# Leftover taps, distances and leftover coefficients regrouped on TensorE, and the batch norms' rows moved by one round, in a two-layer graph network kernel

## The chip, the cores and the metric

The kernel runs on one core of one Trainium2 chip. A core has five engines with instruction streams of their own: TensorE (PE, matrix products; its weight loads are shown as PEld), VectorE (DVE), ScalarE (ACT), GpSimd (POOL) and SyncE (SP, which here only issues DMAs). [...] The metric is the device time of one execution in microseconds; less is better. Everything is computed in float32, and each float32 product shows in the trace as two passes, so a "x2" in a row of TensorE is one product of the program.

## The reference

Two layers over 128 graphs of 128 nodes with 256 features each:

```python
# layer 0, per graph
norm  = (adj.sum(-1) + 1e-6) ** -0.5
f_hom = norm * (adj @ (norm * (x @ theta)))
gate  = sigmoid(x @ W_t + b_t)
x = layernorm(x + elu(gate * f_hom + (1 - gate) * (x @ W_h)))
# layer 1, with adj as a mask of weights
h = relu(bn1(conv1(x.T)))                  # kernel size 1
h = bn2(conv1d(h, conv2_w, pad=8))         # 17 taps along the nodes
x_conv = relu(h + x.T).T
s = x @ w_se.T + b_se                      # 3 coordinates per node
dist = |s_n|^2 + |s_m|^2 - 2 s_n . s_m
x_nmp = (exp(-dist) * adj) @ relu(x @ w_msg.T + b_msg)
x = layernorm(x + gru(concat(x_conv, x_nmp), x))
```

## The kernel before

The graphs are taken in 64 pairs and later in 32 groups of four (`G = 4`). The 17-tap convolution is done by a real Fourier transform of length 136: analysis of `h` with a 128x136 table `A`, one product over the features per frequency, and synthesis back. Of the 136 coefficients the first 128 fill the array's rows and the last `ML = 8` are "leftovers" that are kept apart everywhere: `S` is the 128x128 way back and `SL` the one of the leftovers.

**Stage A** (0 to about 740 us) walks over the pairs in rounds `t`, software-pipelined: in round `t` `l0_project` of pair `t`, the gate and the norm of pair `t-1`, `l1_turn` and `l1_front` of `t-2`, `l1_analyse` of `t-3`, `l0_turn` of `t+1`, `l0_mix` of `t`. In every second round it also transforms a part of the convolution's weights: `w_unit(u)` loads two features in each of four 32-row groups (17 taps in 32 rows), multiplies each group by the table `T` (four products `w_ps`, L416, which stand in four separate row groups of the array), and makes the 8 leftover coefficients of all four groups by one more product over all 128 rows, `wl_ps` (L419), with a block-diagonal table `TL`. VectorE copies the leftovers out (L425). `w_store` writes all of it to `w_d` in DRAM a round later, eight DMAs for the main part (L433) and eight of 8 KB for the leftovers (L438), all on SP's queue. From round 3 on the order of PE, SP, DVE and ACT is the program's own; in rounds up to 2 only PE's is, and a scheduler orders the others.

In round 0 `batch_norms` transposes the norms' vectors (`vec_ps`), makes scale and shift (POOL takes the power), builds diagonal matrices (L227), spreads them over all partitions by one product (`row_ps`, L229) and scales `conv1_w` with it. `table` makes `A` and `T` on VectorE. `way_back` in round 1 makes `S`, `SL` and `TL`. POOL also computes each pair's reciprocal square roots: `inv_sqrt` (L161, L162), for the degrees and for the layer norms (`rstd_a`), in one queue.

**Stage B** (about 740 to 921 us) loops over 68 pairs of coefficients: it loads 512 KB of `w_d` per step (`wb`, L647), makes `y_ps` (L652) and `z_ps` (L665), and writes `y_d`. `others` prepares the next stage's constants in between, among them `mask`.

**Stage C** (from 921 us) walks over the 32 groups `g`: `l1_gather(g)` (the messages, `nmp_ps`), for `g+1` `l1_own` (POOL writes a masked copy `own` of 128x512, L814, from the transposed distance factors `turned`) and `l1_project` (`msg_ps`), `l1_gru(g, 0)`, then `l1_kernel(g+1)` (one product `dist_ps` of 128 rows by 512 columns, L824, its exponential on ACT, L828, and the product with the adjacency on VectorE, L829), in every second step `l1_synth` of the next two groups, and `l1_gru(g, 1)`. `l1_synth` makes 16 products with `S` (L752) and then 16 with the leftovers (L760, 8 rows each, in four row groups side by side), into four banks of the pool `acc`; VectorE takes them out (L769). `l1_gru` has seven `product`s of six passes of 384 columns (L899), in the order 0, 1, 5, 6, 4, 3, 2, each into one of four banks of the pool `psC`. PE's order is the program's; the other engines' is the scheduler's.

Of the kernel before, what the change touches and what calls it, by code (L numbers as in the profile page):

```python
# [14 lines left out]
P = 128  # L15
# [7 lines left out]
GD = P // KD  # L23
PAD = TAPS // 2
# [9 lines left out]
def gnn_layers_kernel(ctx: ExitStack, tc: tile.TileContext, a: dict, out: bass.AP):  # L34
# [54 lines left out]
    TL = taps.tile([P, 4 * ML], F32, tag="TL", name="TL")  # L89
# [9 lines left out]
    io = apool("io", 4, reuse_waits="tile")  # L99
    wk = apool("wk", 1, reuse_waits="tile")  # L100
    wf = apool("wf", 1, reuse_waits="tile")
    ps = actx.enter_context(tc.tile_pool(name="psA", bufs=8, space=PSUM, reuse_waits="tile"))
# [51 lines left out]
    for t in wt:  # L154
        nc.vector.memset(t, 0.0)
# [57 lines left out]
    def batch_norms():  # L213
        n = 2 * NC
        tv = bank("vec_ps")
        nc.tensor.transpose(tv[:, 0 : 4 * n], vec, ident[0 : 4 * n, 0 : 4 * n])
        col = setup.tile([P, 4 * n], F32, tag="col", name="col")
        nc.vector.tensor_copy(col, tv[:, 0 : 4 * n])
        inv_sqrt(scale, col[:, 0:n], BN_EPS, n)
        nc.vector.tensor_mul(scale, scale, col[:, 2 * n : 3 * n])  # L220
        nc.vector.tensor_mul(shift, col[:, n : 2 * n], scale)
        nc.vector.tensor_sub(shift, col[:, 3 * n : 4 * n], shift)

        diag = setup.tile([P, n, P], F32, tag="diag", name="diag")
        for i, v in enumerate((scale, shift)):
            for c in range(NC):
                nc.vector.tensor_scalar(diag[:, NC * i + c, :], ident, v[:, c : c + 1], None, ALU.mult)  # L227
        tr = bank("row_ps")
        nc.tensor.matmul(tr, lhsT=ones, rhs=diag.rearrange("p a b -> p (a b)"), start=True, stop=True)  # L229
        nc.vector.tensor_copy(shift1, tr[:, D : 2 * D])  # L230
        for c in range(NC):
            nc.vector.tensor_mul(conv1_w[:, c, 0:D], conv1_w[:, c, 0:D], tr[:, 0:D])

    def way_back():

        AL = setup.tile([P, P], F32, tag="AL", name="AL")
        nc.gpsimd.memset(AL, 0.0)
        nc.gpsimd.memset(TL, 0.0)
        back = setup.tile([P, 1], F32, tag="back", name="back")
        nc.vector.memset(back, 2.0 / L)  # L240
        nc.vector.memset(back[0:2], 1.0 / L)
        for r, (lo, hi) in enumerate(quarters):
            nc.vector.tensor_copy(TL[lo:hi, r * ML : (r + 1) * ML], T[lo:hi, P:M])
            nc.vector.tensor_copy(AL[:, lo : lo + ML], A[:, P:M])
        tS = bank("S_ps")
        nc.tensor.transpose(tS[:, 0:P], A[:, 0:P], ident)
        nc.tensor.transpose(tS[:, P : 2 * P], AL, ident)
        nc.vector.tensor_scalar(S, tS[:, 0:P], back, None, ALU.mult)
        nc.vector.tensor_scalar(SL, tS[:, P : 2 * P], 2.0 / L, None, ALU.mult)
# [126 lines left out]
    def l1_front(p):  # L376
        s = st[p]
        h = s["h"] = wf.tile([P, J, D], F32, tag="h", name=f"h_{p}")
        for j in range(J):
            ph = bank(f"conv1_ps_{p}_{j}")  # L380
            for c in range(NC):
                nc.tensor.matmul(  # L382
                    ph[:, 0 : D + CO], lhsT=s["x1T"][:, c, nodes(j)], rhs=conv1_w[:, c, :],
                    start=(c == 0), stop=(c == NC - 1),
                )
            nc.vector.tensor_tensor(h[:, j, :], ph[:, 0:D], shift1, ALU.add)
            nc.scalar.activation(coords[:, p * J + j, :], ph[:, D : D + CO], AF.Copy)
        nc.scalar.activation(h, h, AF.Relu)
# [22 lines left out]
    def w_unit(u):  # L411
        t = wt[u % NW].rearrange("p i o -> p (i o)")
        pq = [bank(f"w_ps_{u}_{r}") for r in range(4)]
        for r in range(4):
            k = slice(32 * r, 32 * r + TAPS)
            nc.tensor.matmul(pq[r], lhsT=T[k, 0:P], rhs=t[k, :], start=True, stop=True)  # L416
        pl = bank(f"wl_ps_{u}")
        wo = s_w[u] = []
        nc.tensor.matmul(pl[0 : 4 * ML, :], lhsT=TL, rhs=t, start=True, stop=True)  # L419
        for r in range(4):  # L420
            o = taps.tile([P, 2, D], F32, tag="wo", bufs=4, name=f"w_o_{u}_{r}")
            nc.scalar.activation(o.rearrange("p i o -> p (i o)"), pq[r], AF.Copy)
            wo.append(o)
        ol = taps.tile([4 * ML, 2, D], F32, tag="wl", name=f"wl_o_{u}")
        nc.vector.tensor_copy(ol.rearrange("p i o -> p (i o)"), pl[0 : 4 * ML, :])  # L425
        wo.append(ol)

    def w_store(u, between=lambda: None):
        *wo, ol = s_w.pop(u)
        for r in range(4):  # L430
            f = r * QF + 2 * u
            for i in range(2):
                nc.sync.dma_start(w_d[0 : P // 2, f + i, :, :], wo[r][:, i, :])  # L433
        between()
        for r in range(4):
            f = r * QF + 2 * u
            for i in range(2):
                nc.sync.dma_start(w_d[P // 2 : M // 2, f + i, :, :], ol[r * ML : (r + 1) * ML, i, :])  # L438
# [32 lines left out]
    units = {2 + u * (NP - 3) // (NU - 1): u for u in range(NU)}  # L471
    hstack = ExitStack()
    H = None
    E = mybir.EngineType
    for t in range(-1, NP):
        with tc.manual_schedule(engines={E.PE, E.SP, E.DVE, E.Activation} if t > 2 else {E.PE}):
# [15 lines left out]
            if t == 0:  # L492
                batch_norms()
                table(A, node, "A")
                table(T, lag, "T")

                cos, sin = T[:, 2:M:2], T[:, 3:M:2]
                both = setup.tile([P, M // 2 - 1], F32, tag="both", name="both")
                nc.vector.tensor_sub(both, sin, cos)
                nc.vector.scalar_tensor_tensor(sin, sin, -1.0, cos, ALU.mult, ALU.subtract)  # L500
                nc.vector.tensor_copy(cos, both)
# [7 lines left out]
            if t - 1 in units:  # L509
                w_store(units[t - 1])  # L510
            on(t + 1, l0_turn)
            if t == 3:
                nc.scalar.dma_start(w_msg, a["w_msgT"].rearrange("(c p) e -> p c e", p=P))
                nc.scalar.dma_start(b_msg, a["L1_gnn_b_msg"].partition_broadcast(P))
            if t == 1:
                way_back()
# [3 lines left out]
            on(t, l0_mix)  # L520
            if t in units:
# [5 lines left out]
    with tc.manual_schedule(engines={E.PE, E.SP, E.DVE, E.Activation}):  # L527
# [10 lines left out]
        w_store(units[last], lambda: m_load(3))  # L538
# [35 lines left out]
    mask = cw.tile([P, GD], F32, tag="mask", name="mask")  # L574
# [4 lines left out]
    def others():  # L579
# [18 lines left out]

        mask_i = cw.tile([P, GD], I32, tag="mask_i", name="mask_i")
        nc.gpsimd.iota(mask_i, pattern=[[-KD, GD]], base=0, channel_multiplier=1)  # L600
        mask_f = cw.tile([P, GD], F32, tag="mask_f", name="mask_f")
        nc.vector.tensor_copy(mask_f, mask_i)
        nc.vector.tensor_scalar(mask, mask_f, 0.0, None, ALU.is_ge)
        nc.vector.scalar_tensor_tensor(mask, mask_f, float(KD - 1), mask, ALU.is_le, ALU.mult)
# [79 lines left out]
    acc = cpool("acc", 4, space=PSUM)  # L684
# [44 lines left out]
    def load_y(d):  # L729

        yl = cy.tile([P, G, P], F32, tag="yl", bufs=2, name=f"yl_{d}")
        for e in range(2):
# [3 lines left out]
            for c in range(NC):  # L736
                r = NC * e + c
                nc.sync.dma_start(
                    yl[32 * r : 32 * r + ML],
                    y_d[g * G : (g + 1) * G, P:M, c * P : (c + 1) * P].rearrange("q m f -> m q f"),  # L740
# [4 lines left out]
    def l1_synth(d):  # L745
        pcs = {}
        for e in range(2):
            s = st[2 * d + e]
            for c in range(NC):
                pc = pcs[e, c] = acc.tile([P, 512], F32, tag="acc", name=f"conv2_ps_{2 * d + e}_{c}")  # L750
# [5 lines left out]
        for q in range(G):  # L756
            for e in range(2):
                for c in range(NC):
                    k = slice(32 * (NC * e + c), 32 * (NC * e + c) + ML)
                    nc.tensor.matmul(  # L760
                        pcs[e, c][:, nodes(q)], lhsT=sy[2 * d + e][1][k, q, :], rhs=SL[k, :],
                        start=False, stop=(q == G - 1), skip_group_check=True,
                    )
# [36 lines left out]
    def l1_own(g):  # L800
        if g % (GD // G) == 0:
# [10 lines left out]
        own = ck.tile([P, G, P], F32, tag="own", name=f"own_{g}")  # L812
        lo = g * G % GD
        nc.gpsimd.tensor_tensor(  # L814
            own, turned[:, 1, :].unsqueeze(1).to_broadcast([P, G, P]),
            mask[:, lo : lo + G].unsqueeze(2).to_broadcast([P, G, P]), ALU.mult,
# [3 lines left out]
    def l1_kernel(g):  # L820
        s = st[g]
        turned, own = s["turned"], s["own"]
        pd = bankc(f"dist_ps_{g}")
        nc.tensor.matmul(  # L824
            pd, lhsT=turned[:, 0, :], rhs=own.rearrange("p q n -> p (q n)"), start=True, stop=True
        )
        AT = ck.tile([P, G * P], F32, tag="AT", name=f"AT_{g}")
        nc.scalar.activation(AT, pd, AF.Exp, scale=-1.0)  # L828
# [62 lines left out]
    def l1_gru(g, pr):  # L891
# [3 lines left out]

        def product(i):
            pg = bankc(f"g_ps_{g}_{pr}_{i}")
# [44 lines left out]
    with tc.manual_schedule(engines={mybir.EngineType.PE}):  # L942
# [6 lines left out]
        for g in range(2):  # L949
            l1_project(g)  # L950
        for g in range(2):
            l1_kernel(g)
        l1_factors()
        l1_synth(0)
        for g in range(NG):
# [11 lines left out]
            if 2 <= g + 1 < NG:  # L967
                l1_kernel(g + 1)
            if g % 2 == 1 and d + 1 < ND:
                l1_synth(d + 1)  # L970
            if g + 1 < NG:
                l1_gru(g, 1)
# [44 lines left out]
```

## Time and profile before

| | us |
|---|---|
| median of 3 timed runs (2067.38 to 2068.47) | 2068.39 |
| the profiled execution, its own time | 2071.49 |
| its span, first to last instruction | 2069.7 |
| TensorE busy in the span | 2040.8 |
| VectorE, ScalarE, GpSimd busy | 1440.8, 745.3, 669.3 |

In the profile a row gives the line, the engine, the operation and its output and inputs. The chain of waits follows the work that ended last back from the end; each line is a start, a duration in us, and what ran. The timeline lists instructions by start and duration, with the idle time of the engine ahead of them in brackets. `issue` stands for time in which an engine waited for nothing that the profile shows, and `SPq` for the queue in which SP issues DMAs.

### The profile page before, as it was taken

The page shows a single profiled execution, that of the slowest core. Times are in us where ns is not written, and L with a number is a line of the kernel's source. Part 1 is how long each engine was busy: PE and PEld are TensorE (multiplying, and loading weights), DVE is VectorE, ACT ScalarE, POOL GpSimd, SP SyncE. Part 2 cuts the span into 40 slices and gives each one's busy share as a digit, 9 for nine tenths or more (in the row PEclk, how much of TensorE's full clock was granted, in tenths as well). Part 3 has the DMA queues.
Part 4 walks back from the last instruction along what each step waited for, and adds up shares of the span by engine and source line. Part 5 has one row for each costly group of instructions (what it writes and reads, how often), then busy time and mean ns, then how long its engine had stood idle before and what let it go on. Part 6 is the DMA issues. An engine that isn't in the chain of part 4 may idle for free.

```text
span 2069.7 us, 27486 instructions
## 1 busy us (share of the span) xinstructions
PE 2040.8 (99%) x9025; PEld 1401.2 (68%) x9025; DVE 1440.8 (70%) x2865; ACT 745.3 (36%) x1488; POOL 669.3 (32%) x889
## 2 busy tenths in 40 slices
PE   8999999999999999999999999999999999999997
PEld 5676676676666678886666666666666666666664
DVE  7777777777777754447776777676767767666766
ACT  3555565555555521112222222222222222222222
POOL 1111111111111135463443434343434434443431
PEclk9999999999999999999999999999999999999999
DMA  3444344344344379994222112212212221221100
GB/s 118 142 149 139 131 150 138 129 154 137 130 153 135 128 265 357 311 300 141 78 73 70 59 63 74 77 52 75 75 51 78 73 68 57 68 73 57 37 26 21
DMA packets 193533, 238.54 MB, mean 115 GB/s; under 512 B 16608, under 2 KB 136944, under 8 KB 193392
## 3 DMA queue, kind: packets, MB, share of 16 engines
q1 hardware_dynamic: 187040, 231.02, 33.9%
q10 hardware_dynamic: 6352, 5.78, 0.9%
q8 instruction: 72, 1.18, 0.3%
q14 instruction: 69, 0.57, 0.1%
HBM read 131.87 MB, written 104.86 MB: 114 GB/s over the span
## 4 chain that ended last, share of the span: by engine, by line
PE 95%; DVE 2%; DMA 2%; ACT 1%; issue 0%; SPq 0%; POOL 0%; POOLq 0%; ACTq 0%; DVEq 0%
PE g_ps L899 41%; PE f_ps L312 10%; PE conv_ps L382 5%; PE gate_ps L317 5%; PE y_ps L652 5%; PE msg_ps L788 5%; PE mix_ps L338 3%; PE coef_ps L400 3%; PE nmp_ps L839 3%; PE conv_ps L752 3%; PE z_ps L665 3%; PE w_ps L416 2%; PE x1T_ps L279 2%; PE wl_ps L419 1%; PE xT_ps L279 1%; PE dist_ps L824 1%
## 5 line engine op out<-in xcount | busy, mean ns | idle before, releaser
L312 PE MATMUL f_ps<-w,xT 128*128 128x512 f32 x512 | 242.6, 596 | 0.1
L865 ACT ACTIVATE o<-o 128x1024 f32<-128x1024 f32 (+1 forms) x65 | 67.9, 1044 | 328.0 <-DVE o L935 279.6
L161 POOL TENSOR_SCALAR rstd_b<-mv_b 128x2 f32<-128x2 f32 (+1 forms) x65 | 12.6, 194 | 501.3 <-DVE mv_b L257 501.3
L161 POOL TENSOR_SCALAR rstd_a<-mv_a 128x2 f32<-128x2 f32 x64 | 12.3, 193 | 456.1 <-DVE mv_a L257 456.1
L899 PE MATMUL g_ps<-t_h,sh 128*128 128x384 f32 x384 | 155.3, 486 | 0.0
L899 PE MATMUL g_ps<-t_c,sc 128*128 128x384 f32 x384 | 155.2, 486 | 0.0
L899 PE MATMUL g_ps<-t_m,sm 128*128 128x384 f32 x384 | 155.2, 486 | 0.0
L266 ACT ACTIVATE y<-y,nb_b,rstd_b 128x256 f32<-128x256 f32 x128 | 70.0, 593 | 227.3 <-DVE nb_b L264 226.8
L317 PEld LDWEIGHTS gate_ps<-w,xT 128*128 128x128 f32 x512 | 97.9, 191 | 68.5 <-issue 61.3
L652 PE MATMUL y_ps<-wb,H 128*128 128x256 f32 x544 | 129.7, 381 | 4.5 <-DMA wb<-w_d 2.8
L317 PE MATMUL gate_ps<-w,xT 128*128 128x256 f32 x512 | 132.1, 381 | 0.0
L312 PEld LDWEIGHTS f_ps<-w,xT 128*128 128x128 f32 x512 | 88.4, 192 | 62.3 <-issue 61.8
L321 ACT ACTIVATE hom<-f_ps,norm 128x256 f32<-128x256 f32 x128 | 60.7, 474 | 190.4 <-PE f_ps L312 190.4
L932 POOL TENSOR_TENSOR u<-u,p 128x512 f32<-128x512 f32 x63 | 79.8, 1267 | 149.5 <-DVE p L916 149.5
L660 POOL TENSOR_TENSOR ws<-wb 128x512 f32<-128x512 f32 x67 | 92.9, 1387 | 95.2 <-PE z_ps L665 47.1
L382 PE MATMUL conv_ps<-conv_w,x1T 128*128 128x259 f32 x512 | 122.5, 381 | 0.0
L652 PEld LDWEIGHTS y_ps<-wb,H 128*128 128x128 f32 x544 | 103.6, 191 | 19.8 <-issue 4.6
L788 PE MATMUL msg_ps<-w_msg,cx1T 128*128 128x256 f32 x480 | 108.4, 379 | 0.0
L899 PEld LDWEIGHTS g_ps<-t_h,sh 128*128 128x128 f32 x384 | 72.8, 190 | 51.2 <-issue 1.8
L899 PEld LDWEIGHTS g_ps<-t_c,sc 128*128 128x128 f32 x384 | 73.0, 190 | 50.9
L899 PEld LDWEIGHTS g_ps<-t_m,sm 128*128 128x128 f32 x384 | 73.0, 190 | 50.9 <-DVE sm L854 0.2
L382 PEld LDWEIGHTS conv_ps<-conv_w,x1T 128*128 128x128 f32 x512 | 97.2, 190 | 14.5
(227 smaller groups left out, 4637.1 us busy)
## 6 DMA issues: line engine op xcount, KB each, us to landing
wb<-w_d SPq DMA_DIRECT2D x68, 512.0 KB
w_d<-w_o SPq DMA_DIRECT2D x256, 128.0 KB
y_d<-yb SPq DMA_DIRECT2D x68, 256.0 KB
x<-in_x SPq DMA_DIRECT2D x64, 256.0 KB
cx1T<-x1T_d SPq DMA_DIRECT2D x64, 256.0 KB
yt<-y_d SPq DMA_DIRECT2D x32, 512.0 KB
cx<-x_d SPq DMA_DIRECT2D x32, 512.0 KB
x_d<-x SPq DMA_DIRECT2D x63, 256.0 KB
```

Of the source, the lines that this page charges most:

```text
L266: nc.scalar.activation(dst[:, q, :], src[:, q, :], AF.Identity, bias=nb[:, q : q + 1], scale=rstd[:, q : q + 1],)
L279: nc.tensor.transpose(t[:, (c * J + j) * P : (c * J + j + 1) * P], src[:, j, c * P : (c + 1) * P], ident,)
L312: nc.tensor.matmul(pf, lhsT=xT[:, c, nodes(j)], rhs=w0[:, c, 0 : 2 * D], start=(c == 0), stop=(c == NC - 1),)
L317: nc.tensor.matmul(pg[:, j * D : (j + 1) * D], lhsT=xT[:, c, nodes(j)], rhs=w0[:, c, 2 * D : 3 * D], start=(c == 0), stop=(c == NC - 1),)
L338: nc.tensor.matmul(pm[:, j * D : (j + 1) * D], lhsT=adjT_[:, j, :], rhs=hom[:, j, :], start=True, stop=True,)
L382: nc.tensor.matmul(ph[:, 0 : D + CO], lhsT=s["x1T"][:, c, nodes(j)], rhs=conv1_w[:, c, :], start=(c == 0), stop=(c == NC - 1),)
L652: nc.tensor.matmul(py[:, blk, :], lhsT=coefs(blk if k == 0 else 2 * k + 1 - blk, c), rhs=w[:, c, blk, :], start=(c == 0), stop=(c == NC - 1),)
L660: nc.gpsimd.tensor_tensor(ws, w[:, :, 0, :], w[:, :, 1, :], ALU.add)
L788: nc.tensor.matmul(pm[:, j * D : (j + 1) * D], lhsT=x1T[:, c, nodes(q)], rhs=w_msg[:, c, :], start=(c == 0), stop=(c == NC - 1),)
L865: nc.scalar.activation(rz, rz, AF.Tanh, scale=0.5)
L899: nc.tensor.matmul(pg[:, lo : lo + 3 * P], lhsT=s[f"f{kind}"][i][:, pr, :], rhs=factors[kind][i], start=(k == 0), stop=(k == 2), skip_grou ...
L932: nc.gpsimd.tensor_tensor(u4, u2, p5, add)
```

## The change

Five things change together.

- **Leftover taps.** `TL` becomes a table of 119 rows (7 features by 17 taps) by 56 columns, so one product makes the leftovers of 14 features (two sets of 7). The weights are loaded a second time for it, as 119 full rows (`v_load`), and `wl_ps` leaves `w_unit`: 19 units `v_unit` take the place of 32 products, in rounds without a `w_unit`. `v_store` writes four DMAs of 28 rows per unit. `TL` is filled by 14 small DMAs that POOL issues, where VectorE copied four blocks.
- **Distances.** The coordinates are kept in another order of graphs, so that the four graphs of a group stand in four 32-row groups. `own` becomes one 128x128 product by a column of `mask` on VectorE; `dist_ps` becomes four products of 32 rows by 128 columns, in four row groups and four banks of `acc`. `acc` becomes one buffer of four banks that the distances and `l1_synth` share.
- **Leftover coefficients.** The four graphs' 8 leftovers fill 32 rows, and `SLb`, made by four VectorE products in stage B, holds a masked `SL` for each graph: four products of 32 rows by 512 columns in place of sixteen of 8 rows by 128.
- **The batch norms' rows** (diagonals, `row_ps`, scaling) run in round 1 instead of round 0.
- **Order.** `l1_kernel(g+1)` runs inside `l1_gru(g, 1)`, ahead of the fifth product; the pool `io` is placed behind `wk` and `wf`, the three memsets of `wt` go, and in the last round the leftovers' stores no longer stand between `w_store` and stage B's loads on SP.

```diff
     def way_back():
-        AL = setup.tile([P, P], F32, tag="AL", name="AL")
-        nc.gpsimd.memset(AL, 0.0)
-        nc.gpsimd.memset(TL, 0.0)
+        AL = setup.tile([P, P // ML, ML], F32, tag="AL", name="AL")
+        nc.vector.tensor_copy(AL, A[:, P:M].unsqueeze(1).to_broadcast([P, P // ML, ML]))
+        nc.vector.memset(TL, 0.0)
...
-        for r, (lo, hi) in enumerate(quarters):
-            nc.vector.tensor_copy(TL[lo:hi, r * ML : (r + 1) * ML], T[lo:hi, P:M])
-            nc.vector.tensor_copy(AL[:, lo : lo + ML], A[:, P:M])
+        cols = TL.rearrange("p (r i k) -> p r i k", r=2, i=FS)
+        for i in range(FS):
+            for r in range(2):
+                nc.gpsimd.dma_start(
+                    cols[i * TAPS : (i + 1) * TAPS, r, i, :], T[0:TAPS, P + r : M : 2]
+                )
...
     def w_unit(u):
...
-        nc.tensor.matmul(pl[0 : 4 * ML, :], lhsT=TL, rhs=t, start=True, stop=True)
...
+    def v_load(v):
+        t = taps.tile([P, 2, D], F32, tag="vt", bufs=2, name=f"v_t_{v}")
+        for i, (f, n) in enumerate(v_sets(v)):
+            nc.sync.dma_start(
+                t[0 : n * TAPS, i, :], a["conv2_wT"][f : f + n].rearrange("i t o -> (i t) o")
+            )
+        s_v[v] = t
+    def v_unit(v):
+        n, sets = v_sets(v)[-1][1] * TAPS, len(v_sets(v))
+        pl = bank(f"wl_ps_{v}")
+        nc.tensor.matmul(
+            pl[0 : ML * FS, 0 : sets * D], lhsT=TL[0:n],
+            rhs=s_v[v][0:n, 0:sets].rearrange("p i o -> p (i o)"), start=True, stop=True,
+        )
+        ol = s_v[v] = taps.tile([ML * FS, 2, D], F32, tag="wl", name=f"wl_o_{v}")
+        nc.vector.tensor_copy(
+            ol[:, 0:sets].rearrange("p i o -> p (i o)"), pl[0 : ML * FS, 0 : sets * D]
+        )
...
             if t == 0:
-                batch_norms()
+                norms = batch_norms()
+                next(norms)
...
             if t == 1:
+                next(norms, None)
                 way_back()
...
-        w_store(units[last], lambda: m_load(3))
+        w_store(units[last])
+        m_load(3)
...
+        for q in range(G):
+            nc.vector.tensor_scalar(SLb[:, q, :], SL, mask[:, q : q + 1], None, ALU.mult)
...
-    acc = cpool("acc", 4, space=PSUM)
+    acc = cpool("acc", 1, space=PSUM)
...
     def l1_synth(d):
+        four = acc.tile([P, 4, 512], F32, tag="acc", name=f"conv2_ps_{d}")
...
+                nc.tensor.matmul(
+                    pcs[e, c], lhsT=sy[2 * d + e][1][k, :],
+                    rhs=SLb[k].rearrange("p q n -> p (q n)"),
+                    start=False, stop=True, skip_group_check=True,
+                )
...
     def l1_own(g):
-        nc.gpsimd.tensor_tensor(
-            own, turned[:, 1, :].unsqueeze(1).to_broadcast([P, G, P]),
-            mask[:, lo : lo + G].unsqueeze(2).to_broadcast([P, G, P]), ALU.mult,
-        )
+        nc.vector.tensor_scalar(
+            own, turned[:, 1, :], mask[:, g % GR : g % GR + 1], None, ALU.mult
+        )
...
     def l1_kernel(g):
-        pd = bankc(f"dist_ps_{g}")
-        nc.tensor.matmul(
-            pd, lhsT=turned[:, 0, :], rhs=own.rearrange("p q n -> p (q n)"), start=True, stop=True
-        )
+        pd = acc.tile([P, G, 512], F32, tag="acc", name=f"dist_ps_{g}")
+        for q in range(G):
+            k = slice(q * P // G, (q + 1) * P // G)
+            nc.tensor.matmul(
+                pd[:, q, 0:P], lhsT=turned[k, 0, :], rhs=own[k, :], start=True, stop=True
+            )
...
             l1_gru(g, 0)
-            if 2 <= g + 1 < NG:
-                l1_kernel(g + 1)
             if g % 2 == 1 and d + 1 < ND:
                 l1_synth(d + 1)
             if g + 1 < NG:
-                l1_gru(g, 1)
+                l1_gru(g, 1, {4: lambda: l1_kernel(g + 1)})
```

## The prediction

> **What bounds the kernel.** I read the page's busy shares first, then the chain of waits for TensorE's pace in each stage, then the timeline where that chain leaves TensorE.
>
> ```profile
> PE 2040.8 (99%) x9025; PEld 1401.2 (68%) x9025; DVE 1440.8 (70%) x2865; ACT 745.3 (36%) x1488; POOL 669.3 (32%) x889
> PE 95%; DVE 2%; DMA 2%; ACT 1%; issue 0%; SPq 0%; POOL 0%; POOLq 0%; ACTq 0%; DVEq 0%
> ```
>
> TensorE is the bound nearly everywhere, so TensorE time taken out is time gained, except at the start and between stages A and B, where it waits. Its prices, from the chain:
>
> ```profile
> 40.34 1.07 PE w_ps L416 x8
> 41.41 0.98 PE wl_ps L419 x2
> ...
> 72.56 1.75 PE conv_ps L382 x8
> 84.79 1.75 PE conv_ps L382 x8
> 94.81 1.75 PE conv_ps L382 x8
> ...
> 985.25 1.10 PE conv_ps L760 x32
> 986.36 13.74 PE g_ps L899 x42
> ...
> 1015.43 0.86 PE dist_ps L824 x2
> 1016.29 13.54 PE g_ps L899 x42
> ```
>
> A round with weights takes 84.79 - 72.56 = 12.23 us, one without 10.02: the weights cost 2.21, of which 0.98 is the leftover product. A distance product costs 0.86. The 32 passes of the leftover coefficients, four side by side, take 1.10, and what follows takes 13.74 instead of 13.54, so 1.30 in all.
>
> The two places where TensorE waits, in the timeline:
>
> ```profile
> 9.08 7.21 SPq L125 DMA_DIRECT2D wt<-in_conv_wT  x8
> 17.59 1.70 PE L229 MATMUL row_ps<-diag,ones 128*128 128x512 f32 x2 [3.39 <-DVE diag L227]
> 28.78 0.19 POOL L161 TENSOR_SCALAR rstd_a<-mv_a 128x2 f32<-128x2 f32 x1 [6.64 <-DVE mv_a L257]
> 30.64 0.33 PE L279 MATMUL x1T_ps<-ident,x 128*128 128x128 f32 x1 [1.43 <-ACT x L266]
> ...
> 731.01 5.07 SPq L438 DMA_DIRECT2D w_d<-wl_o  x8
> 743.99 2.73 PE L652 MATMUL y_ps<-wb,H 128*128 128x256 f32 x8 [2.08 <-DMA wb<-w_d]
> [...]
> ```
>
> [...]
>
> **Part by part.**
>
> *Leftover taps.* 32 products at 0.98 go (31.4 us); 18 of the same 512 columns and one of half that come, 18 x 0.98 + 0.55 = 18.2. That is -13.2. Less, if part of the 0.98 is the way out of the row groups and stays with `w_ps`: four passes' worth of streaming is 4 x 0.43 = 1.72 of the 2.21 (`f_ps` of the same width: four passes in 1.72), so 0.49 is switching; all of it left with `w_ps` gives 32 x 1.35 + 18 x 0.86 + 0.43 = 59.1 against 70.7, -11.6. If the product with 56 columns pays such a switch of its own, 19 x 0.41 comes on top: about -4. I take -12.0, range -4 to -13.2. The copies (0.68 on VectorE) fall from 32 to 19 and lie in rounds where VectorE has about 2.5 us free (481.7 busy of 640 us in stage A). On SP's queue 256 stores and their issues fall to 76, and 38 loads are added, 4.5 MB; DMA engines are 43% busy there. Nothing.
>
> *Distances.* New cost, by the leftover coefficients' row: 32 passes four side by side are 8 x 0.11 = 0.89 us of streaming (0.11 from 3.57 us for 32 passes of L752), so going into row groups and out costs 1.30 - 0.89 = 0.41. A distance is two such steps: 0.22 + 0.41 = 0.63 instead of 0.86. 32 x -0.23 = -7.4. With no switching cost it would be -0.64 each, -20; with 0.64 of it, nothing. [...]
>
> *Leftover coefficients.* Four side by side already: eight steps of 128 columns become two of 512, the same 1024 columns, plus the 0.41: 1.27 against 1.30. 16 x -0.03 = -0.5, between -1.6 and +1.6 (0.1 each way). `SLb` is four VectorE products of about 0.28 us (`diag`, 128x128) in stage B, where VectorE is under half busy.
>
> *`own` on VectorE.* POOL loses 32 x 1.12 us, VectorE gains 32 x 0.28 = 9 in a stage where it is busy 750 of 1070 us: hidden under `g_ps`, nothing; at worst 9 if all of it delayed a copy that TensorE waits for.
>
> *The move of `l1_kernel`.* After it only three products lie ahead of the gather, 18 passes x 0.3226 = 5.8 us. In them: the exponential (0.58), the VectorE product (0.69), and what is queued ahead of them: one layer-norm statistic or three copies, about 2 us. Hidden, with about 2.5 to spare. The exponential stands behind two ReLUs on ACT that wait for the same copies out of `acc`. The shared `acc` adds one wait, in the odd groups; see the second rival.
>
> *The batch norms' rows.* In round 0 TensorE's 3.39 idle and 1.70 of product go; the product lands in round 1, where TensorE waited 1.43 + 0.16 anyway. The first mix moves from 20.8 to 15.7. From the mix to the first `x1T_ps` the chain took 9.85 us; VectorE adds four diagonals and the broadcast `AL`, about 1.2. So `x1T_ps` could start at 26.8 to 27.0 instead of 30.64: -3.6.
>
> *The 14 DMAs on POOL.* This is the price that the trace doesn't have: POOL issues none before. They wait for the finished `T` (about 17.1 us, a `xT` copy now being ahead of its last step on VectorE) and stand in POOL's queue ahead of the first `rstd_a`, with one `inv_sqrt` (0.9) among them. With c per DMA POOL is free at 18.0 + 14 c; from there to `x1T_ps` it took 30.64 - 28.78 = 1.86. So the first `x1T_ps` stands at 19.9 + 14 c, if that is later than 27.0. Rows for c: the shortest issue on SP or ACT, 0.33; 0.90 for the `wt` loads of 17 strided rows at this same time; 1.12 for POOL's own 128x512 operation, 1.49 at its longest. I take 1.0, between the two nearest: 33.9, or +3.2 against before. Ends: -3.6 (0.33) and +10.1 (1.49). [...]
>
> *Stage A to B.* SP's queue loses the eight leftover stores (5.07 us) between the main stores and the loads of `wb`, which then start at about 732 instead of 737.3 and land (6.47) before 739.94, when TensorE is ready. The 2.08 idle goes; the two steps after it took 1.9 us more than the usual 2.59 each, of which I take half; and `early_ps` no longer waits 0.55 for a bank. -2.1 - 1.0 - 0.6 = -3.7, between -1 and -5.5. What is late next is ACT's end of stage A (1.71 idle ahead of the first `y_ps`), which stays. `io`'s new place changes what stage B's buffers wait for, not TensorE's chain.
>
> **Sum:** +3.2 - 12.0 - 7.4 - 0.5 - 3.7 = -20.4. The profiled execution had 2071.49, so 2051.1 for one like it; it stood 3.1 above the median, so 2068.39 - 20.4 = **2048.0**.
>
> **Rivals.**
>
> 1. *POOL's DMAs are cheap*, 0.5 us or less: the start gives 3.6 instead of costing 3.2: 2041. For it: SP's and ACT's issues of 0.33 to 0.5. Against: POOL does in 0.7 us a power of 128x2, and 68 single elements per DMA are many.
> 2. *The shared `acc` holds the distances.* In odd groups `dist_ps` needs the four copies of `l1_synth` out of the banks. Before, in the round from 1106 us, these end at 1132.2; without the adjacency product (0.6) ahead of them about 1131.6. The distance comes 24 passes after the synthesis, 1124.8 + 7.7 = 1132.5. 0.9 to spare. If the copies came 2 us later, 15 groups x 1.1 = 16.5 us: 2064. A TensorE gap ahead of the fifth product would show it.
> [...]
>
> [...]
>
> **Numbers.** Forecast 0.55, rival 1 0.17, c near 2 0.15, rival 2 0.07, rival 3 0.06. 0.2% (4.1 us) is about what a measurement of this kernel can tell from no change. Faster: all of the first two, most of the third, half of rival 2: 0.86; within 0.2%: 0.05; slower: 0.09. The range goes from rival 1 with the distances at -13 (2036) to rival 2 and the slow start (2064).
>
> **What would show it.** Right: no `wl_ps` in rounds with `w_ps`, a `dist_ps` group near 0.6 us, no SP leftover stores ahead of `wb`, the first `x1T_ps` near 34 us with a wait that ends at POOL. Wrong: `x1T_ps` near 27 or 59, a wait ahead of `dist_ps` in odd groups, `nmp_ps` waiting for `AT`, or 56-column products above 1.1 us.

## The result and the profile after

The changed kernel takes 2052.82 us (median of 4 runs, 2050.97 to 2053.39) against 2068.43 for the kernel before in the same session (2067.38 to 2068.82): a ratio of 0.9924, 95% interval 0.9907 to 0.9941, that is 15.6 us faster. The forecast was 20.4 us less, 2048.0, with a range from 2036 to 2064. The profiled execution of the changed kernel took 2053.39 us, 18.1 less than that of before (2071.49); the trace's times below stand against that 18.1.

On the page, the busy time of the engines and the share of the engines in the chain that ended last:

```profile
PE 2023.9 (99%) x8807; PEld 1384.2 (67%) x8807; DVE 1432.1 (70%) x2882; ACT 746.4 (36%) x1488; POOL 652.0 (32%) x869
PE 96%; DVE 2%; POOL 1%; DMA 1%; ACT 0%; issue 0%; POOLq 0%; DVEq 0%; ACTq 0%; SPq 0%
```

TensorE has 16.9 us less to do and still bounds the kernel. POOL's share of the chain rises from 0% to 1%.

The chain of waits in stage A, three rounds (start, duration, what):

```profile
77.52 1.75 PE conv_ps L387 x8
...
81.02 1.07 PE w_ps L423 x8
82.09 0.59 PE x1T_ps L284 x4
...
88.77 1.75 PE conv_ps L387 x8
...
92.27 1.00 PE wl_ps L455 x2
93.27 0.59 PE x1T_ps L284 x4
...
99.94 1.75 PE conv_ps L387 x8
```

A round with `w_ps` now takes 88.77 - 77.52 = 11.25 us, one with the seven-feature `wl_ps` 99.94 - 88.77 = 11.17, and one with neither 10.03. So the main taps cost 1.22 and a leftover product 1.15: 1.00 for itself and the rest on the transposes behind it (0.59 where a plain round has 0.44).

The same view in stage C, a distance and then the leftover coefficients:

```profile
948.45 0.43 PE dist_ps L880 x8
948.88 6.00 PE g_ps L964 x18
...
970.22 3.57 PE conv_ps L808 x32
973.79 1.07 PE conv_ps L815 x8
974.86 7.94 PE g_ps L964 x24
```

Eighteen passes of `g_ps` take 5.81 us elsewhere and 6.00 behind the distance, so a distance costs 0.43 + 0.19 = 0.62 us instead of 0.86. Behind the coefficients 24 passes take 7.94 instead of 7.74: 1.07 + 0.20 = 1.27 instead of 1.30. TensorE shows no wait at all between 920 and 2040 us.

The start, in the timeline (start, duration, engine, line, what; in brackets the idle time ahead and what ended it):

```profile
8.59 7.08 SPq L127 DMA_DIRECT2D wt<-in_conv_wT  x8
15.72 1.35 SPq L116 DMA_DIRECT2D x<-in_x  x1
20.22 12.63 POOL L247 DMA_DIRECT2D TL<-T  x12
25.86 1.09 PE L284 MATMUL xT_ps<-ident,x 128*128 128x128 f32 x4 [4.97 <-DMA x<-in_x]
32.93 0.19 POOL L161 TENSOR_SCALAR rstd_a<-mv_a 128x2 f32<-128x2 f32 x1
34.80 1.40 PE L284 MATMUL x1T_ps<-ident,x 128*128 128x128 f32 x4 [3.48 <-ACT x L271]
35.99 3.62 PE L317 MATMUL f_ps<-w,xT 128*128 128x512 f32 x4
43.70 1.91 PE L387 MATMUL conv_ps<-conv_w,x1T 128*128 128x259 f32 x8
```

POOL goes straight from its last `TL` DMA to `rstd_a`; then comes the first `x1T_ps`, at 34.80 instead of 30.64. Two things beside it were not in the forecast. The third pair's `x` lands late, and TensorE waits 4.97 us for it; in the kernel before it came to this product only at 27.13 and found `x` there. And after the waits TensorE is slow: the four passes of `f_ps` take 3.62 us here and 1.88 in the row of before at the same place. Before, in the timeline:

```profile
27.13 0.60 PE L279 MATMUL xT_ps<-ident,x 128*128 128x128 f32 x4
...
31.52 1.88 PE L312 MATMUL f_ps<-w,xT 128*128 128x512 f32 x4
...
36.68 1.91 PE L382 MATMUL conv_ps<-conv_w,x1T 128*128 128x259 f32 x8
```

The windows of the changed kernel say why. Their columns are the stretch, its length, the busy time and number of instructions of PE, PEld, DVE, ACT and POOL, and then the granted clock, the DMA share and GB/s:

```profile
20.00:25.00 5.00, 0.89 (x5) 0.43 (x3) 2.73 (x7) 2.54 (x6) 5.00 (x6) 0.90 0.75 123
25.00:30.00 5.00, 4.14 (x13) 3.03 (x14) 1.25 (x4) 0.00 (x0) 5.00 (x6) 0.50 0.66 18
35.00:40.00 5.00, 4.98 (x10) 2.55 (x10) 3.42 (x8) 0.51 (x2) 0.00 (x0) 0.50 0.49 143
```

Behind a stretch with 0.89 us of work the granted clock is 0.50, and again behind the 3.48 us of waiting. From the first `x1T_ps` to the first `conv_ps` the kernel before took 36.68 - 30.64 = 6.04 us; this one takes 43.70 - 34.80 = 8.90.

Between stages A and B, in the timeline:

```profile
721.36 5.08 SPq L434 DMA_DIRECT2D w_d<-w_o  x8
...
729.86 2.04 SPq L703 DMA_DIRECT2D wb<-w_d  x4
734.69 3.69 PE L708 MATMUL y_ps<-wb,H 128*128 128x256 f32 x16 [0.76 <-ACT H L411]
```

No stores of leftover rows stand between the main stores and the loads of `wb`, `y_ps` does not wait for `wb` any more, and TensorE's idle time in this stretch falls from 4.5 to 1.3 us.

Stage by stage, profile against profile:

| stretch | forecast | measured |
|---|---|---|
| start, to the first `conv_ps` | +3.2 | +7.0 (36.68 to 43.70) |
| stage A, first `conv_ps` to last `mix_ps` | -12.0 (taps) | -10.1 (682.63 to 672.55) |
| last `mix_ps` to first `turn_ps` | -3.7 | -6.6 (202.87 to 196.31), of which 1.05 is the last round's `wl_ps`, counted in the forecast under the taps |
| first `turn_ps` to the end | -7.9 | -8.5 (1147.5 to 1139.0) |
| sum | -20.4 | -18.1 (2069.7 to 2051.6; the rows are rounded) |

### The profile page after: what moved, and what is told of

Same layout as the page of the kernel before. It is cut to its first block, busy times and chain, and to the rows that moved or that the text cites. A ratio compares the mean times of both kernels' runs of the same rounds, so it can differ in the third digit from the quotient of the medians.

```text
span 2051.6 us, 27050 instructions
## 1 busy us (share of the span) xinstructions
PE 2023.9 (99%) x8807; PEld 1384.2 (67%) x8807; DVE 1432.1 (70%) x2882; ACT 746.4 (36%) x1488; POOL 652.0 (32%) x869
## 4 chain that ended last, share of the span: by engine, by line
PE 96%; DVE 2%; POOL 1%; DMA 1%; ACT 0%; issue 0%; POOLq 0%; DVEq 0%; ACTq 0%; SPq 0%
PE g_ps L964 42%; PE f_ps L317 11%; PE conv_ps L387 5%; PE gate_ps L322 5%; PE msg_ps L844 5%; PE y_ps L708 5%; PE mix_ps L343 3%; PE coef_ps L407 3%; PE nmp_ps L897 3%; PE conv_ps L808 3%; PE z_ps L721 3%; PE x1T_ps L284 2%; PE w_ps L423 2%; PE xT_ps L284 1%; PE deg L297 1%; PE wl_ps L455 1%
## 5 line engine op out<-in xcount | busy, mean ns | idle before, releaser
L161 POOL TENSOR_SCALAR rstd_b<-mv_b 128x2 f32<-128x2 f32 (+1 forms) x65 | 18.2, 280 | 529.6 <-DVE mv_b L262 529.6
L964 PE MATMUL g_ps<-w_hhT_w,cx1T 128*128 128x384 f32 x256 | 105.0, 492 | 0.0
```

Of the source, the lines that this page charges most:

```text
L964: nc.tensor.matmul(pg[:, lo : lo + 3 * P], lhsT=s[f"f{kind}"][i][:, pr, :], rhs=factors[kind][i], start=(k == 0), stop=(k == 2), skip_grou ...
```

## The experiments

All but the last are the changed kernel with one part or two altered; the last is the kernel before with one line moved. Times are medians, ratios are against the kernel before in the same session with the 95% interval, and "first `conv_ps`" is the mark of the start: 36.68 us before, 43.70 after.

### The 14 DMAs replaced by a TensorE product

`T`'s 17 rows are copied to 119 rows by a product with a 17x119 spread of the identity, and VectorE masks them into `TL`.

```diff
-                nc.gpsimd.dma_start(
-                    cols[i * TAPS : (i + 1) * TAPS, r, i, :], T[0:TAPS, P + r : M : 2]
-                )
+        nc.tensor.matmul(tT[0:n, 0:ML], lhsT=spread..., rhs=T[0:TAPS, P:M], ...)
+        for r in range(2):
+            nc.vector.tensor_tensor(cols[0:n, r], tT[0:n, r:ML:2]..., block..., ALU.mult)
```

> TL is filled by one small TensorE product (17 rows spread to 119) and two masked VectorE copies; POOL issues no DMA. Theory: the 14 DMAs in POOL's queue (1.06 us each) hold the first rstd_a until 32.9 us, so the first x1T_ps stands at 34.8, and the clock that TensorE loses in the wait costs 2 to 3 us more behind it. Without them rstd_a comes at about 25, x1T_ps at about 27, the first conv_ps of L387 at about 33.5 instead of 43.9: 2043 us against the changed kernel's 2053. Rival: the third pair's x lands at 25.9 us anyway (SP's queue is late), the mix and x1T_ps then come at about 31, and the gain is 4 us: 2049.

2045.62 us (2043.97 to 2046.16), ratio 0.989 [0.9877, 0.9904]: 7.2 less than the changed kernel. In the timeline:

```profile
24.99 0.63 PE L300 MATMUL xT_ps<-ident,x 128*128 128x128 f32 x4 [3.12 <-DMA x<-in_x]
30.46 1.06 PE L300 MATMUL x1T_ps<-ident,x 128*128 128x128 f32 x4
37.16 1.92 PE L403 MATMUL conv_ps<-conv_w,x1T 128*128 128x259 f32 x8
```

The DMAs cost 7.2 us, not the 10 that the theory gave, and the first `conv_ps` stands about where it stood before the change. The wait for `x` is what remains, as the rival had it, but it takes back less than the rival said.

### The 14 DMAs on SP's queue

```diff
-                nc.gpsimd.dma_start(
+                nc.sync.dma_start(
```

> The same 14 DMAs with single elements, issued by SP instead of POOL. Theory of POOL's queue: as e1, x1T_ps at about 27 and 2043 us, since what held the norm was the issuing. Rival, the 952 four-byte elements fill the DMA engines and make the third pair's x late: xT_ps of that pair still waits until about 26, x1T_ps comes at about 31, and the time is 2047 to 2049.

2053.17 us (2052.05 to 2053.65), ratio 0.9927 [0.9915, 0.994]: no different from POOL. In the timeline:

```profile
26.44 14.54 SPq L247 DMA_DIRECT2D TL<-T  x14
...
34.95 1.91 PE L387 MATMUL conv_ps<-conv_w,x1T 128*128 128x259 f32 x8
45.62 1.39 PE L284 MATMUL x1T_ps<-ident,x 128*128 128x128 f32 x4 [5.94 <-ACT x L271]
54.17 1.91 PE L387 MATMUL conv_ps<-conv_w,x1T 128*128 128x259 f32 x8
```

and two of the 14 in the chain of waits:

```profile
30.98 2.65 SPq L247
33.67 0.62 SPq L247
```

Neither expectation held. The 14 hold SP for 14.54 us, 1.04 each on average, about as long as they hold POOL. But they are not alike there: the first two take 4.48 us together, the third 2.65 and the other eleven 0.62 each, where POOL takes 1.06 for nearly every one; why the first three take so long, no run shows. The first round goes through early, at 34.95, but now the store of `x` stands behind the 14 in SP's queue, and the chain of the second round runs through that store. TensorE waits 5.94 us one round later, and the second `conv_ps` is at 54.17, where the changed kernel has it at 54.94. The hold moved to another queue and another round.

### The batch norms' rows back in round 0

```diff
                 next(norms)
+                next(norms, None)
...
-                next(norms, None)
                 way_back()
```

> The changed kernel with the batch norms' rows back in round 0. Theory: the start ends at POOL's queue, which hangs on T and not on the rows; x1T_ps stays at 34 to 36 and the time within 1.5 us of the changed kernel's 2053, so moving the rows brought nothing here. Rival, the step of the prediction (the move takes 3.6 us out of the start): 2056 to 2057.

2051.14 us (2050.31 to 2052.56), ratio 0.9919 [0.9905, 0.9933]; first `conv_ps` at 41.28. So beside POOL's DMAs the move of the rows brings nothing. If anything it costs 1.7 us, which can't be told from nothing: TensorE's idle 3.64 ahead of `row_ps` lies earlier than a wait that would come anyway.

### The product, and the rows back

> e1 with the batch norms' rows back in round 0. Theory: with POOL's queue free the rows matter, as the prediction's step had it: x1T_ps at about 30.6 as before the change, 3.6 us more than e1. Rival: something else sets the start in e1 as well, and e4 equals e1 within 1 us.

2046.73 us (2045.78 to 2047.2), ratio 0.9895 [0.988, 0.9911], first `conv_ps` at 36.73 against 37.16 without the rows' return. In the median that is 1.1 us more, a little over the rival's 1 us and not to be told from nothing. The theory that the rows are worth 3.6 us fell here as well. In the timeline:

```profile
17.63 1.59 PE L230 MATMUL row_ps<-diag,ones 128*128 128x512 f32 x2 [3.43 <-DVE diag L228]
```

The 3.43 us wait for the rows is back, but in the place of the 3.12 us wait for the third pair's `x`: TensorE comes to that product only at 27.17 us and does not wait there. So without the rows in round 0 another wait sets the start, the one for `x`. On SP that load stands behind the eight loads of `wt` (the first two lines of the timeline of the start above). Whether that is the cause is for the next two.

### The product, and the tap weights loaded later

```diff
     load(1)
-    w_load(0)
-    w_load(1)
...
                     load(t + 2)
+                    if t == 1:
+                        w_load(0)
+                        w_load(1)
```

> The leftover taps by one TensorE product, and the eight loads of the tap weights behind the fourth pair's load on SP instead of ahead of the third's. Theory (with the 14 DMAs gone, the start is set by the third pair's x, which stands behind those eight loads on SP, 7.5 us of issue): the third pair's xT_ps goes at about 21.5 instead of 25.0, with no wait for x, the TensorE's idle time ahead of it is gone, and the median is 2041.5 to 2043 (2045.6 before this step). Rival (it is late for another reason: the load takes long, or the x1T chain through VectorE and ACT sets the start): the median stays within 2045 to 2047.

2043.26 us (2042.17 to 2044.27), ratio 0.9878 [0.9863, 0.9893], the fastest of all, 0.3 above the theory's range and well below the rival's. In the timeline:

```profile
20.38 0.60 PE L298 MATMUL xT_ps<-ident,x 128*128 128x128 f32 x4
25.22 0.33 PE L298 MATMUL x1T_ps<-ident,x 128*128 128x128 f32 x1 [1.40 <-ACT x L285]
31.25 1.92 PE L401 MATMUL conv_ps<-conv_w,x1T 128*128 128x259 f32 x8
37.60 0.33 PE L298 MATMUL x1T_ps<-ident,x 128*128 128x128 f32 x1 [1.61 <-ACT x L285]
```

The theory holds: the third pair's `xT_ps` goes at 20.38 without a wait, and the clock stays at 1.00 in every window of 5 us from 15 to 45. The first `conv_ps` is 5.9 us earlier, the third 3.8 (55.81 against 59.65), since the next `x1T_ps` now waits. In the median 2.4 us is left.

### The same, with the rows back

> The same, with both batch norms' rows in the first round as in the kernel before. Theory (the prediction's 3.6 us for the rows are real once no load is late): 3 to 4 us longer than the kernel with the taps late alone. Rival (the rows' wait runs beside another wait here as well): within 1.2 us of it.

2046.46 us (2045.82 to 2047.42), ratio 0.9894 [0.988, 0.9907]: 3.2 us more, as the theory had it. In the timeline:

```profile
16.55 2.08 PE L228 MATMUL row_ps<-diag,ones 128*128 128x512 f32 x2 [3.43 <-DVE diag L226]
```

With no load late, the 3.43 us wait ahead of `row_ps` now costs about its length. The forecast's 3.6 us for the rows is real, but only there.

### The changed kernel with the tap weights loaded later

The same move of `w_load`, with the DMAs on POOL as they are.

> The changed kernel with its 14 DMAs on POOL as they are, and only the tap weights' loads moved behind the fourth pair's load. Theory (the 14 DMAs hold the norms' chain until 33 us, whatever x does): the third pair's xT_ps goes earlier, at 21 to 22, the idle time moves behind it, ahead of x1T_ps, which stays at 34 to 35; the median is 2052 to 2054. Rival (the late x cost time beside the DMAs, through the drop of the granted clock): 2048 to 2051.

2051.84 us (2050.87 to 2052.65), ratio 0.9919 [0.9906, 0.9933]: 1.0 less than the changed kernel, 0.16 below the theory's range, and not to be told from no change. In the timeline:

```profile
34.25 1.39 PE L282 MATMUL x1T_ps<-ident,x 128*128 128x128 f32 x4 [11.08 <-ACT x L269]
...
42.91 1.91 PE L385 MATMUL conv_ps<-conv_w,x1T 128*128 128x259 f32 x8
```

`x` is there, and all of TensorE's idle time now lies in one piece ahead of `x1T_ps`, which starts at 34.25, 0.55 us earlier than it did. The late `x` does not set the start while POOL's DMAs are there. The slow clock comes with the wait for POOL: it is 0.50 from 30 to 40 us, and `x1T_ps` to `conv_ps` takes 8.66 us here, 8.90 in the changed kernel.

### The leftover taps as before

`TL` in quarters, a `wl_ps` in every round with `w_ps`, and no `v_load`, `v_unit`, `v_store`. The 14 DMAs go with it; the memsets of `wt` and the leftovers' stores of the last round ahead of stage B's loads come back. The rest is as changed.

```diff
-            for r in range(2):
-                nc.gpsimd.dma_start(...)
+        for r, (lo, hi) in enumerate(quarters):
+            nc.vector.tensor_copy(TL[lo:hi, r * ML : (r + 1) * ML], T[lo:hi, P:M])
```

> The changed kernel with the leftover taps as they were (32 products in w_unit, 256 stores of 8 KB, TL by VectorE copies, no DMA on POOL). Theory: the taps' products cost 10 us more in stage A, the last round's stores bring about 5 us back between the stages, and the start loses its 10 us of POOL queue and slow clock: 2053 + 10 + 5 - 10 = 2058, x1T_ps at about 27. Rival, the start is set by something else: 2068.

2057.2 us (2056.94 to 2059.13), ratio 0.9952 [0.9939, 0.9964]: 4.4 more than the changed kernel, as the theory had it. The first `conv_ps` is 9.4 us earlier (34.29), stage A costs what it cost before the change, and ahead of stage B the wait for `wb` is back:

```profile
740.44 1.97 PE L668 MATMUL y_ps<-wb,H 128*128 128x256 f32 x8 [0.95 <-DMA wb<-w_d]
```

So the new taps pay at their place, and give most of it back at the start.

### The distance as one product again

`own` as a 128x512 product on POOL, `dist_ps` as one product of 128 rows by 512 columns, still in the shared `acc`.

```diff
-        for q in range(G):
-            nc.tensor.matmul(pd[:, q, 0:P], lhsT=turned[k, 0, :], rhs=own[k, :], ...)
+        nc.tensor.matmul(pd[:, 0, :], lhsT=turned[:, 0, :], rhs=own.rearrange("p q n -> p (q n)"), ...)
```

> The changed kernel with the distances as one product of 128 rows by 512 columns again (own 128x512 on POOL, masked to one 32-row block per graph); place, order of the graphs and the shared acc stay. Theory: going into row groups and out costs 0.41 us, so four side by side take 0.63 against 0.86 and the row groups are worth 32 x 0.23 = 7.4 us: 2060. Rival A, no switching cost shows in the sum: 20 us, 2073. Rival B, the gain came from the new place and not from the row groups: 2053.

2062.83 us (2061.92 to 2064.27), ratio 0.9975 [0.9966, 0.9984]: 10.0 us more, where the theory had 7.4. The products are 32 x (0.86 - 0.62) = 7.7 of it. The other part is in the first group, in the timeline:

```profile
916.58 2.40 POOL L869 TENSOR_TENSOR own<-turned,hit 128x512 f32<-128x512 f32 x2
918.03 1.43 PE L879 MATMUL dist_ps<-own,turned 128*128 128x512 f32 x2 [2.15 <-POOL own L869]
919.26 5.04 PE L844 MATMUL msg_ps<-w_msg,cx1T 128*128 128x256 f32 x16
```

TensorE waits 2.15 us for POOL's `own`, and the 16 passes of `msg_ps` behind that wait take 5.04 us where 16 take 3.62 in the changed kernel. Together that is 11.3 us, somewhat more than the 10.0 of the medians and the 10.8 of the two spans. In the kernel before, the first distance stood behind all 32 passes of the messages; the changed order puts it behind 16, and `own` on VectorE is in time for that.

### The distance at its old place

```diff
             l1_gru(g, 0)
+            if g + 1 < NG:
+                l1_kernel(g + 1)
             if g % 2 == 1
...
-            l1_gru(g, 1, {4: lambda: l1_kernel(g + 1)})
+            l1_gru(g, 1)
```

> The changed kernel with l1_kernel(g+1) back between l1_gru(g, 0) and l1_synth. Theory: with one acc the synthesis of the odd groups then waits for the exponential of the distances (0.58 us, and 1.06 more where a tanh stands ahead of it on ScalarE): 0.7 to 2 us in 15 groups, 10 to 30 us, 2063 to 2083; even groups nothing. Rival: TensorE has other work or the exponential comes at once, 2053 within 3 us, and the move was not needed.

2102.14 us (2100.57 to 2103.85), ratio 1.0166 [1.0153, 1.018]: 49 more than the changed kernel, well over what either side expected. The timeline of one odd group:

```profile
968.78 0.50 PE L880 MATMUL dist_ps<-own,turned 32*128 32x128 f32 x8
971.34 5.46 PE L808 MATMUL conv_ps<-S,yt 128*128 128x128 f32 x32 [2.05 <-ACT AT L884]
```

and the line of the waits of TensorE in stage C:

```profile
PE conv_ps L808 <- ACT AT L884: 30.8, 15, 2.1
```

`acc` has one buffer, so the synthesis, which follows at once, must wait until ACT has read the distances out of it: 15 waits, 30.8 us. In the group shown the clock is down behind it (0.73 in the window from 970 to 975 us, 0.55 from 973 to 976; over the whole run its mean is 0.986, in the changed kernel 0.995), and the busy time of the synthesis grows from 59.7 to 79.2 us. Together 50.3 us, against 48.4 more of span. The slow clock was left out of the expectations and is 40% of the cost.

### The pool `io` ahead of `wk` and `wf` again

```diff
+    io = apool("io", 4, reuse_waits="tile")
     wk = apool("wk", 1, reuse_waits="tile")
     wf = apool("wf", 1, reuse_waits="tile")
-    io = apool("io", 4, reuse_waits="tile")
```

> The changed kernel with the pool io ahead of wk and wf again. Theory: the place of io changes only which buffers stage B's first outputs wait for; TensorE's chain between the stages hangs on the last norm and on wb: 2053 within 1.5 us. Rival: the first zb waits for the stores of the early messages again (7.6 us on ScalarE before the change) and TensorE with it: 2 to 5 us more.

2060.07 us (2058.68 to 2060.42), ratio 0.9961 [0.9948, 0.9973]: 7.3 more. The theory of no effect is wrong. On TensorE and VectorE, in the timeline:

```profile
742.18 0.76 DVE L718 TENSOR_TENSOR hs<-H 128x256 f32<-128x256 f32 x2 [6.47 <-DMA msg_d<-early]
742.75 2.04 PE L721 MATMUL z_ps<-ws,hs 128*128 128x256 f32 x4 [6.05 <-DVE hs L718]
```

With `io` at its old place stage B's `hs` waits until the store of the early messages has landed, and TensorE waits 6.05 us for `hs`. Behind the wait it is slow: the four passes of `z_ps` take 2.04 us where they take 1.03 in the changed kernel. That `hs` lies over tiles of the early messages follows from the order of the pools in the code; the trace shows the wait only.

### The kernel before with only `io` moved

The same line moved in the kernel before.

> The kernel before, with only the pool io moved behind wk and wf. Theory (io's old place makes stage B's first buffers wait for the early messages' stores, but in the kernel before that wait runs beside the wait for the last leftover row's store and the load of wb, which is as long): 2066.5 to 2068.5, that is, 0 to 1.9 us gained. Rival (the place of io is worth by itself what its return cost in the changed kernel, 7.3 us): about 2061.

2067.27 us (2066.32 to 2070.64), ratio 0.9997 [0.9988, 1.0006]: no difference, as the theory had it. In the timeline TensorE still waits for `wb`:

```profile
743.44 1.97 PE L652 MATMUL y_ps<-wb,H 128*128 128x256 f32 x8 [1.04 <-DMA wb<-w_d]
```

In the kernel before, the store of the early messages held `zb` on ScalarE and not `hs`, and TensorE did not wait with it:

```profile
748.46 0.39 ACT L670 ACTIVATE zb<-z_ps 128x256 f32<-128x256 f32 x1 [7.61 <-DMA msg_d<-early]
```

So what `io`'s place is worth depends on the rest. By the profiles, the stretch from the last `mix_ps` to the first `turn_ps` takes 202.87 us before, 204.62 in the changed kernel with `io` at its old place, where the leftover stores are out of the way already, and 196.31 with both changes: to take the leftover stores away alone brings nothing there. With only `io` moved it is 198.13, but the profiled execution of before stood 3.1 us above its median and this one 0.3 below, and the medians show 1.0.

## Why the prediction was right or wrong

**The direction and the mechanism were right**: TensorE's own time fell, and the start took part of it back. The size was 4.8 us off by the medians and 2.3 by the profiles, within the range. By the profiles the start came out 3.8 us and stage A with its taps 0.9 us worse than forecast, the way from stage A to B 1.8 and stage C 0.6 better; that these partly cancel is luck.

*The 14 DMAs on POOL: the price was right, the sum behind it not.* The price c was taken as 1.0 us; the trace has 12 in 12.63, 1.05 each, and the first `x1T_ps` came at 34.80 for 33.9. What failed is the step from there: the forecast let everything behind the first `x1T_ps` run at its old pace, and it ran at a granted clock of 0.50 from 35 to 40 us and 0.89 from 40 to 45. Of the 7.0 us at the start, 3.2 was forecast, 0.9 is the later `x1T_ps`, and 2.9 the slower way to `conv_ps` (8.90 instead of 6.04). With the late `x` taken away most of the last two stays (34.25, and 8.66 from there).

*The rows' -3.6: right as a size, wrong as a term of this kernel.* The move alone shows 3.2 us where no load is late, and nothing that can be told beside POOL's DMAs or with the late `x`. The forecast did take the later of two ends (27.0 and 19.9 + 14 c), so its +3.2 did not rest on the rows, but its best case did: "POOL's DMAs are cheap, 2041" overlooked the load of the third pair's `x` behind the eight `wt` loads, whose line the prediction shows. Without any DMA the kernel stands at 2045.62, and at 2043.26 with that load freed.

*Leftover taps, -12.0: the term was mis-sized.* 2.21 to 1.22 in 32 rounds is -31.7, as good as the whole 0.98 of the old product. The new product is what was priced too low: 18 at 1.15, for the 0.98 or less that was taken, and one of half the columns at 0.72 are 21.4, so -10.3. Each lone product is followed by transposes that take 0.15 more (0.59 for 0.44). The prediction named such a cost of the new product, at 0.41 each, and gave it hardly any weight in its -12.0. The stage's own -10.1 and the 1.05 of the last round are 0.8 more than -10.3, and that is no matter of the taps: in the kernel before an `x1T_ps` at 65.44 us waits 0.65 us for ScalarE and the next one 0.17, and in the changed kernel TensorE waits nowhere between 44 and 716 us. What took that wait away is not shown; with the old taps in the changed kernel it is there (0.61 and 0.16).

*Distances, -7.4, and coefficients, -0.5: right to 0.01 and 0.00 us each* (0.62 for 0.63, 1.27 for 1.27). The 0.41 for going into row groups and out, an estimate from the leftover coefficients' row (1.30 - 0.89), carried over: 0.62 less the 0.22 of streaming is 0.40. The whole step came out at 0.86 / 0.62 = 1.4x, the rows of `dist_ps` alone (0.43 for 0.86) at 2x. What TensorE does in the 0.40, no row shows.

*`own` on VectorE: nothing, right*, and more useful than said: on POOL it would now hold the first distance (2.15 us).

*The move of `l1_kernel` and the shared `acc`: right.* TensorE does not wait in stage C, so the second rival's 0.9 to spare was enough. The return to the old place shows what the same buffer costs the other way round, when the synthesis waits for the distances: 2.05 us per odd group, and two thirds as much again in the slower passes behind the wait (19.5 us to 30.8).

*Stage A to B, -3.7: measured -5.5 by the profiles* (without the leftover product). The 2.08 idle and the 0.55 went as said, the slow steps went whole where half was taken, and the wait for ACT fell from 1.71 to 0.76. But the profiled execution of before, high above its median, seems to hold more of this than most: with the leftover stores in place, the kernel with the old taps and the one with only `io` moved wait 0.95 and 1.04 us for `wb`, not 2.08, and have no slow steps. Against the first of them the changed kernel gains 2.2 us here (199.53 - 1.04 - 196.31). So the 2.5 us between 18.1 by the profiles and 15.6 by the medians may lie in this stretch; no run settles it. The step that failed is the last sentence: "`io`'s new place changes what stage B's buffers wait for, not TensorE's chain". For the kernel before it holds, but in the changed kernel `io` put back costs 7.3 us, with TensorE waiting 6.05 for `hs`. The sum came out by luck in this, since the change contains the move and the forecast gave it no worth.

*The chances for dearer DMAs (c near 2, 0.15, and rival 3, 0.06)* did not come: no run shows POOL near that price. One DMA takes it 1.06 us in the median and 1.28 at most, and on SP's queue, where POOL has no part, the 14 take as long in all (14.54 us).

## What to carry to other kernels

Where several waits end close together, as at a start or between two stages, the chain shows only the last: before a wait is booked as gained, look in each queue for what ends next (a load behind other loads, a buffer that waits for a store). A gap on TensorE can cost more than its length: price in the slow clock behind it, here 1.3 us (the mean behind the 15 gaps of 2.05) to 2.9 us (behind 3.48). The 14 small DMAs held either queue that they were tried on, POOL's at 1.05 us each and SP's at 1.04; where such data is already on the chip, try a product and a masked copy beside other work, which took 7.2 us less here; the version with that and with the tap weights loaded later takes 2043.26 us.

## What the runs showed of the hardware

- A DMA of 68 single elements held POOL for 1.06 us (median of 14, 1.28 at most). On SP eleven of the 14 took 0.62 us and the first three 7.1 together, so that the 14 took 14.54 us in all and the change of queue gained nothing (2053.17 for 2052.82).
- Behind gaps of 2.05 to 4.97 us on TensorE the granted clock was about half for some microseconds. In the changed kernel it was 0.50 from 25 to 30 us, where a gap of 4.97 ends, and 0.50 from 35 to 40, behind one of 3.48, where four `f_ps` passes take 3.62 us instead of 1.88. With the distance at its old place it was 0.55 from 973 to 976 us, behind a gap of 2.05, and 1.00 from 976 to 979; the 32 passes of the synthesis there take 5.46 us instead of 3.73 in the changed kernel. With the product and the tap weights loaded later, where the gaps are 1.40 and 1.61 us, it was 1.00 in every window of 5 us from 15 to 45.
- The four products of 32 rows in separate row groups that make a distance cost 0.62 us where one of 128 rows costs 0.86, that is 0.72 of it. By the estimate from the leftover coefficients' row, 0.41 of the 0.62 is the way into the row groups and out.
